# Layer 2 of a graph network: the tile order turned from low degree first to high degree first

## The chip, the cores and the metric

The kernel runs on one core of one Trainium2 chip. The metric is the device time of one execution in microseconds. A core has five engines that run their own instruction streams in order and meet through semaphores: TensorE (PE, matmuls; PEld is its weight load), VectorE (DVE), ScalarE (ACT), GpSimd (POOL) and SyncE (SP). Here POOL issues all indirect DMAs (gathers and scatters of rows by an index), and SP issues the plain ones.

## The reference, cut to what matters

Four layers run one after the other over 3125 nodes with 256 features each and 50000 edges. Each layer is a graph step and then a feed-forward step, both added to x. The change touches layer 2 and the table that layer 3 gathers from:

```python
# layer 2, graph step: attention over the incoming edges of each node
h_s = h @ W_self.T
z = h @ W_func.T
e = leaky_relu(concat([z[src], z[dst], w]) @ W_att.T)      # one score per edge
alpha = softmax of e over the edges with the same dst
h_new = h_s + segment_sum(alpha * z[src], dst)
x = x + (h + relu(where(deg > 0, h_new, h)))
# layer 2, feed-forward: 16 experts, each node goes to its best 2
gate = x_norm @ gate_w;  top 2, softmax over the two
moe = sum over the two of  w_k * (relu(x_norm @ w1[e] + b1[e]) @ w2[e] + b2[e])
x = x + layernorm(x_norm + moe) * gamma + beta
# layer 3, graph step
xp = relu(x_norm @ W_proj.T + b_proj)
agg = segment_max(xp[src], dst)                            # incoming edges and the node itself
```

## The kernel before, in words

Nodes are sorted by degree, highest first, and the sorted list is cut into 25 tiles of 128 nodes (the last, tile 24, has 53). A tile's number is its degree rank: tile 0 holds the nodes with most incoming edges. `RND` (line 90) gives the number of gather rounds of each tile, from 32 for tile 0 down to 9 for tile 24, 413 in all. One round gathers one neighbour's row for each of the 128 nodes of a tile, with one indirect DMA on POOL (`gather`, line 156).

Layer 2 stands in lines 2375 to 2579. Its work is written as generators (chains) that say which engine they need next and for how long; `Plan.run` (line 1857) plays them against a simple clock of its own and so fixes the order in which each engine's instructions are issued. Among chains that could start at about the same moment the lower rank number goes first. The chains are:

- `own_rows` (rank 0): loads each tile's own x rows into XX, on SP, at most three tiles ahead of the gathers.
- `gathers` (rank 2): the 413 gathers, in blocks of four rounds. There are nine block buffers (`g_rows`, `GR_BUFS`), and a block is free again when its rows are summed.
- `attend` (rank 0): per tile the self matmul (L2469), the scores of all rounds (L2483), the softmax, and the weighted sum, one DVE instruction per round (L2502). A tile's scores need all of its rounds, so its first block comes free only after its last gather.
- `route2` (rank 1): for groups of up to five tiles, layer norm, the gate's logits, top 2, a running count that gives each pick a place in its expert's list, and two scatters per tile (line 160) of the normed rows into the chunk's table xg.
- `ex2.tokens`, `ex2.weights` (rank 0, SP): load an expert's rows from xg once all tiles of the chunk are scattered, and the expert's 1 MB of weights (two halves, two buffers each; in the last chunk, from the third expert on, the weights go into the nine g_rows blocks once the gathers are through with them).
- `experts2` (rank 4): for each chunk the 16 experts one after the other: transposes of the rows (L2196), the hidden matmuls (L2134), relu on ACT (L2222), the output matmuls (L2138), and a store to yg.

The tiles are divided into three chunks (`CH2`, line 96: first tile, end tile, rows per block, blocks). A chunk's table has a fixed number of places per expert: 96 x 2 = 192 for the first two, 128 x 1 for the last. A token that finds no place is counted, and a branch behind the routing (`rest`, line 2299) works such tokens off; it is not taken when there are none, but every engine passes through it.

When the last group is routed, the planner's first run ends, `rest` is issued, and a second run begins in which `experts2` has rank 0. Beside the remaining experts it issues `ex2.fetch` (two gathers per tile of the expert outputs) and `table3`: combine, layer norm, layer norm again, the projection (L2549) and one scatter per tile into layer 3's table tab3. Layer 3's first gather waits for the whole of tab3; layer 3 itself walks the tiles from 0 to 24 and has its own chunks (`CH3`).

The order around the change is this: tiles 24, 23, ... 6 and then 0, 1, ... 5. Chunk 0 is tiles 15 to 24, chunk 1 tiles 6 to 14, chunk 2 tiles 0 to 5.

Of the kernel before, what the change touches and what calls it, by code (L numbers as in the profile page):

```python
# [21 lines left out]
NT = 25  # L22
# [70 lines left out]

CH2 = ((15, 25, 96, 2), (6, 15, 96, 2), (0, 6, 128, 1))
CH3 = ((0, 5, 104, 2), (5, 15, 128, 3), (15, 25, 128, 3))


# [16 lines left out]
def tile_gnn_ffn(ctx: ExitStack, tc: tile.TileContext, a: dict, out: bass.AP):  # L116
# [28 lines left out]
    def bcast(src, n, pool, name):  # L145

        t = pool.tile([P, n], F32, name=name)
        nc.sync.dma_start(t, bass.AP(tensor=src.tensor, offset=src.offset, ap=[[0, P], [1, n]]))
        return t
# [180 lines left out]
    def top2(lg, nt, n, pool, comb):  # L330
        res = {}
        for _ in top2_steps(lg, nt, n, pool, comb, res):
# [13 lines left out]
    xg2, yg2, xg3 = ([dram.tile([places(n, c) + (k[0] == "x") * 2 * P * (c[1] - c[0]), w], F32, name=f"{k}_{i}") for i, c in enumerate(ch)]  # L346
                     for k, n, w, ch in (("xg2", 16, D, CH2), ("yg2", 16, D, CH2), ("xg3", 8, D + TAIL, CH3)))

# [222 lines left out]
    class Search:  # L571
# [14 lines left out]
        def places(self, s):  # L586
            row = self.row[:, s]
            nc.vector.tensor_scalar(row, row, 1.0, None, op0=OP.max)
            nc.vector.tensor_copy(self.rowi[:, s], row)
            nc.vector.tensor_scalar(row, row, float(ET), -float(ET), op0=OP.mult, op1=OP.add)  # L590
# [142 lines left out]
    def first_zeros():  # L733
# [7 lines left out]
        yield  # L741
        for x, n in [(x, places(16, c)) for x, c in zip(xg2, CH2)] + [(x, places(8, c)) for x, c in zip(xg3, CH3)]:
            w = n // P * x.shape[1]
# [1180 lines left out]
    def norm_steps(dst, src, n, pool, pre, ready, twice=False, which=("ACT",)):  # L1924


        st = pool.tile([P, GT, 6], F32, name=pre + "st", bufs=1)
        mv = pool.tile([P, GT, 2], F32, name=pre + "mv", bufs=1)
        nm = pool.tile([P, GT], F32, name=pre + "nm", bufs=1)
        for i in range(n):  # L1930
            f = yield "DVE", 0.41, (ready[i],)
            nc.vector.bn_stats(st[:, i, :], src[:, i, :])  # L1932
            nc.vector.bn_aggr(mv[:, i, :], st[:, i, :])
        s = {}
        f = yield from small_steps(rsq_steps(s, "r", mv[:, :n, 1], n, pool, pre, 1), f)
        r = s["r"]
        if twice:
            v2 = pool.tile([P, GT], F32, name=pre + "v2", bufs=1)
            f = yield "DVE", 0.26, (f,)
            nc.vector.tensor_mul(v2[:, :n], mv[:, :n, 1], r)  # L1940
            nc.vector.tensor_mul(v2[:, :n], v2[:, :n], r)
            f = yield from small_steps(rsq_steps(s, "r", v2[:, :n], n, pool, pre + "2", 1), f)
            f = yield "DVE", 0.08, (f,)
            nc.vector.tensor_mul(s["r"], s["r"], r)
            r = s["r"]
        f = yield "DVE", 0.08, (f,)
        stt(nm[:, :n], mv[:, :n, 0], -1.0, r, op0=OP.mult, op1=OP.mult)
        done = []
        for i in range(n):
            done.append((yield which, 0.58, (f,)))  # L1950
            if plan[0].on == "ACT":
                nc.scalar.activation(dst[:, i, :], src[:, i, :], AF.Identity, bias=nm[:, i : i + 1], scale=r[:, i : i + 1])
            else:
                nc.vector.tensor_scalar(dst[:, i, :], src[:, i, :], r[:, i : i + 1], nm[:, i : i + 1], op0=OP.mult, op1=OP.add)
        return done

    def logit_steps(lg, src, g, w, b, n, ready, R, pool, name, us, *args, **kw):

        last = None
        for i in range(g + 1):  # L1960
            if i < g:
                xt = pool.tile([P, 2, P], F32, name=name, bufs=2)
                xf = yield from turned_steps(R["tp"], xt, src[:, i, :], ready[i], us, *args, **kw)
            if i:
                f = yield "PE", 0.4, (last[1], R["u"])
                free = R["u"].take()
                pl_ = ps("u", [P, 2, D])[:, 0, :n]
                for k in range(2):
                    nc.tensor.matmul(pl_, last[0][:, k, :], w[:, k, :], start=(k == 0), stop=(k == 1))  # L1969
                f = yield "DVE", 0.08, (f + slack[0],)  # L1970
                nc.vector.tensor_add(lg[:, i - 1, :], pl_, b)
                free.t = f
            last = (xt, xf)
        return f
# [400 lines left out]
    with tc.tile_pool(name="g2", bufs=2) as gp, \  # L2375
# [7 lines left out]
        bj = bcast(a["L3_gnn_b_proj"], D, wp, "w_bp")  # L2383
        ex2 = Experts("L2_ffn", 16, AF.Relu, CH2, wp, xg2, yg2)
        q2 = XX[:, :, V_Q + 1]
# [40 lines left out]
                                                   op0=OP.mult, op1=OP.add)  # L2426
        rounds_beyond(wp, body2)

        order2 = list(range(NT - 1, CH2[2][1] - 1, -1)) + list(range(CH2[2][1]))
        pl = plan[0] = Plan()  # L2430
        R = {"tp": Ring(2), "mm": Ring(2), "y": Ring(1), "u": Ring(2), "pu": Ring(1)}
        blocks = Ring(GR_BUFS)
# [3 lines left out]
        def gathers():  # L2436
            for t in order2:
                for r0 in range(0, RND[t], GB):
                    m = min(GB, RND[t] - r0)
                    for r in range(m):  # L2440
                        f = yield "POOL", 1.27, (blocks,) if r == 0 else ()
                        if r == 0:
                            g, free = gp.tile([P, GB, ZW], F32, name="g_rows", bufs=GR_BUFS), blocks.take()
                        gather(g[:, r, :], tab2, srcI[:, OFF[t] + r0 + r : OFF[t] + r0 + r + 1])
                    rows[t].append((r0, m, g, free, f))
                here[t].t = f

        def own_rows():

            for k, u in enumerate(order2):  # L2450
                old = here[order2[k - 3]] if k > 2 else At(0.0)
                while old.t is None:
                    yield None, 0.0, (old,)
                f = yield "SP", 0.45, (old,)
                nc.sync.dma_start(XX[:, u, : V_Q + 2], tabr[u * P : (u + 1) * P, : V_Q + 2])
                xin[u].t = plan[0].moved(f, 4 * P * (V_Q + 2))
# [51 lines left out]
                done[t].t = f  # L2508

        def route2():  # L2510
            for c, t0, g in ((0, 20, 5), (0, 15, 5), (1, 10, 5), (1, 6, 4), (2, 0, 4), (2, 4, 2)):
                s = slice(t0, t0 + g)
                slack[0] = SLACK if c < 2 else 0.0
                ready = yield from norm_steps(XN[:, s, :], X[:, s, :], g, gp, "rn_", [done[t] for t in range(t0, t0 + g)])
                lg = wp.tile([P, GT, 16], F32, name="r_lg")
                f = yield from logit_steps(lg, XN[:, s, :], g, rw2, gb2, 16, ready, R, gp, "r_xt", 0.36)
                yield from ex2.route(c, t0, g, lg[:, :g], f, XN, R)
                for t in range(t0, t0 + g):
                    f = yield "DVE", 0.41, (f,)
                    nc.vector.tensor_add(X[:, t, :], X[:, t, :], be)  # L2520
            moved.t = f

        def experts2():
            for c in range(3):
                yield from ex2.run(c, R)
# [32 lines left out]
        with tc.manual_schedule(engines={EN.PE, EN.DVE, EN.Activation, EN.Pool, EN.SP}):  # L2558
            pl.add(0, own_rows())
            pl.add(2, gathers())  # L2560
            pl.add(0, attend())
            pl.add(1, route2())
            pl.add(0, ex2.tokens())
            pl.add(0, ex2.weights((blocks, lambda: gp.tile([P, GB, ZW], F32, name="g_rows", bufs=GR_BUFS)
                                   .rearrange("p r d -> p (r d)"), here[order2[-1]])))
            ex2.out = "ACT"
            last = pl.add(4, experts2())
            pl.run(moved, R.values())
            ex2.out = "ACT", "DVE"
            ex2.rest(range(NT))  # L2570
            pl.meet(6.0)
            last[0] = 0
            order3 = ((20, 25), (15, 20), (10, 15), (6, 10), (3, 6), (0, 3))
            pl.add(3, ex2.fetch([t for g in order3 for t in range(*g)]))
            befores = [At(0.0), At(0.0)]
            for i, q in enumerate(order3):
                befores.append(At())
                pl.add(3 + i, table3(range(*q), f"t{i % 2}_", befores[i], befores[i + 2]))
            pl.run()
# [193 lines left out]
```

## Time and profile before

| what | value |
|---|---|
| median of 13 runs | 3167.89 us (3160.71 to 3173.7) |
| the profiled execution, its own time | 3165.59 us |
| its span, mean granted PE clock | 3163.9 us, 0.805 |
| PE, PEld, DVE, ACT, POOL busy | 2144.9, 1495.3, 1683.0, 939.7, 1699.0 us |
| layer 2: first gather issued, last gather issued | 1487.2, 2068.0 us |
| layer 3: first gather issued | 2279.7 us |
| 413 gathers of layer 2 on POOL | 404.1 us, 979 ns each |
| sum of one round on DVE (L2502) x413 | 201.5 us, 488 ns each |
| hidden matmuls of layer 2's first two chunks (L2134, 192 columns) and output matmuls (L2138) | 116.9 and 125.3 us with a few of the last chunk's |

A span runs from the first to the last instruction of the profiled execution. Times are microseconds from the span's start. "Busy" leaves out waits; a group's row ends with the idle time of the engine ahead of its instructions and with what ended that idle time. The granted clock is the share of full speed that TensorE was given. The chain that ended last is followed back from the final instruction, at each step to the work that released it.

### The profile page before, as it was taken

What the parts mean: (1) busy time and instruction counts of PE and PEld (TensorE: products, weight loads), DVE (VectorE), ACT (ScalarE), POOL (GpSimd) and SP (SyncE); (2) the same over time, 40 slices, a digit from 0 to 9 for tenths busy, and PEclk for the clock granted to TensorE, in tenths of its full rate; (3) what the DMA queues carried; (4) which work ended last, traced back from release to release, by engine and by line L of the source; (5) the groups of instructions that cost most, each with busy time, mean ns of one, the idle gap of its engine ahead of it and who ended that gap; (6) DMA issues with size and microseconds to landing.
All of it is one profiled execution on the core that took longest, in us unless ns stands there. A gap on an engine that the chain in (4) does not pass through costs nothing. (4 is left out here: it accounts for less than half of the span.)

```text
span 3163.9 us, 35848 instructions
## 1 busy us (share of the span) xinstructions
PE 2144.9 (68%) x10124; PEld 1495.3 (47%) x10124; DVE 1683.0 (53%) x6018; ACT 939.7 (30%) x2059; POOL 1699.0 (54%) x1976
## 2 busy tenths in 40 slices
PE   7999856899999999695223885968311222237898
PEld 3444324556666677574111763757201122226676
DVE  3555245677778875433757565668533333356311
ACT  3555423244444443221101331324100000024343
POOL 2210055466656710423777777754477777747644
PEclk9999976899999999797555896989555555557899
DMA  8999877578888740613433885866233333325665
GB/s 314 377 387 349 319 257 223 170 249 296 290 275 273 237 140 32 216 64 108 138 99 103 256 266 160 271 216 218 67 105 105 105 106 105 105 101 151 162 159 115
DMA packets 244652, 608.06 MB, mean 192 GB/s; under 512 B 47374, under 2 KB 111471, under 8 KB 231498
## 3 DMA queue, kind: packets, MB, share of 16 engines
q0 software_dynamic: 103824, 282.18, 29.8%
q1 hardware_dynamic: 138378, 321.21, 29.6%
q10 hardware_dynamic: 2224, 2.11, 0.2%
q8 instruction: 87, 1.43, 0.2%
q14 instruction: 139, 1.14, 0.1%
HBM read 395.45 MB, written 211.44 MB: 192 GB/s over the span
## 5 line engine op out<-in xcount | busy, mean ns | idle before, releaser
L156 POOL DMA_INDIRECT g<-part,e_code x392 | 378.2, 965 | 420.3 <-DMA f<-in_attr 201.3
L156 POOL DMA_INDIRECT g_rows<-tab,srcI x413 | 404.1, 979 | 129.2 <-issue 101.8
L156 POOL DMA_INDIRECT g_row<-tab,srcI x413 | 391.5, 948 | 131.9 <-issue 118.8
L655 PE MATMUL t<-w_big,n_xt 128*128 128x512 f32 x800 | 355.3, 601 | 11.8 <-DMA w_big<-in_L_gnn_weight 7.1
L2626 DVE TENSOR_TENSOR ACC<-ACC,g_row 128x256 f32<-128x256 f32 x413 | 175.7, 425 | 342.2 <-DMA g_row<-tab,srcI 342.1
L1790 PE MATMUL tp<-ident,ACC 128*128 128x128 f32 x50 | 16.6, 435 | 423.5 <-DVE ACC L2626 423.5
L2134 PE MATMUL mm<-ro_xt,ro_w 128*128 128x192 f32 (+3 forms) x928 | 242.9, 416 | 24.1 <-ACT ro_h L2222 14.6
L655 PEld LDWEIGHTS t<-w_big,n_xt 128*128 128x128 f32 x800 | 151.2, 192 | 195.1 <-issue 175.4
L2138 PE MATMUL y<-ro_w,ro_h 128*96 128x256 f32 (+2 forms) x1040 | 239.9, 384 | 5.0 <-ACT ro_h L2222 5.0
L1021 PE MATMUL w<-xt,w_big 128*128 128x256 f32 (+1 forms) x832 | 216.4, 393 | 0.1
L2134 PEld LDWEIGHTS mm<-ro_xt,ro_w 128*128 128x128 f32 x928 | 183.3, 218 | 69.0 <-ACT ro_h L2222 20.7
L1790 PEld LDWEIGHTS tp<-ident,ACC 128*128 128x128 f32 x50 | 7.2, 203 | 430.8 <-issue 355.3
L2502 DVE SCALAR_TENSOR_TENSOR ACC<-g_rows,g_e,ACC 128x256 f32<-128x256 f32 x413 | 201.5, 488 | 13.3
L1030 PE MATMUL w<-w_big,b_h 128*128 128x256 f32 x800 | 204.1, 392 | 2.9 <-ACT b_h L1023 2.9
L2138 PEld LDWEIGHTS y<-ro_w,ro_h 128*96 128x96 f32 (+2 forms) x1040 | 179.3, 177 | 46.3 <-ACT ro_h L2222 5.9
L893 DVE TENSOR_TENSOR g<-pw,g 128x512 f32<-128x512 f32 x196 | 126.3, 686 | 124.8 <-PE pw L889 87.7
L658 ACT COPY n_tst<-t 128x512 f32<-128x512 f32 x200 | 117.0, 586 | 190.1 <-PE t L655 183.5
L1021 PEld LDWEIGHTS w<-xt,w_big 128*128 128x128 f32 x832 | 149.5, 197 | 50.2 <-issue 27.1
L1030 PEld LDWEIGHTS w<-w_big,b_h 128*128 128x128 f32 x800 | 148.6, 193 | 38.2 <-issue 13.4
L902 PE MATMUL agg<-g,s 128*32 128x256 f32 x1568 | 140.8, 424 | 34.6 <-DMA g<-part,e_code 20.5
L2288 POOL DMA_INDIRECT out_x<-ro_y,ro_at x64 | 101.5, 1585 | 102.4 <-ACT ro_y L2251 92.5
L880 ACT COPY pw<-w_bd 128x512 f32<-128x512 f32 x196 | 112.1, 589 | 115.5 <-DVE g L893 115.0
(600 smaller groups left out, 4200.3 us busy)
## 6 DMA issues: line engine op xcount, KB each, us to landing
part<-n_tst SPq DMA_DIRECT2D x100, 1024.0 KB
ro_w<-in_L_ffn_blocks SPq DMA_DIRECT2D x58, 514.0 KB
ro_w<-in_L_ffn_blocks SPq DMA_DIRECT2D x58, 512.0 KB
part<-p_out SPq DMA_DIRECT2D x98, 256.0 KB
xg<-zero SPq DMA_DIRECT2D x78, 200.0 KB
f<-in_attr SPq DMA_DIRECT2D x49, 256.0 KB
b_at<-in_edge_attr SPq DMA_DIRECT2D x50, 224.0 KB
tabn<-v SPq DMA_DIRECT2D x11, 768.0 KB
```

The source lines that it names most:

```text
L156: return nc.gpsimd.indirect_dma_start(out=dst, out_offset=None, in_=table, in_offset=bass.IndirectOffsetOnAxis(ap=idx, axis=0))
L655: nc.tensor.matmul(pt.rearrange("p r d -> p (r d)"), xt_of[t][:, k, :], wrel[:, k, 2 * i : 2 * i + 2, :].rearrange("p r d -> p (r d)"), st ...
L658: nc.scalar.copy(stage[0][:, o : o + 2, 0, :], pt)
L880: nc.scalar.copy(pw, bd.unsqueeze(1).to_broadcast([P, 2, D]))
L893: nc.vector.tensor_tensor(m, biased.pop(0), m, op=OP.mult)
L902: nc.tensor.matmul(pa[32 * j : 32 * j + 32, h, :], s[:, 2 * j + h, :], rows[4 * g + 2 * (j // 2) + h][:, j % 2, i * D : (i + 1) * D], star ...
L1021: nc.tensor.matmul(ph, w["01"][:, e, k, i * P : (i + 1) * P], xt[:, k, : n * h], start=(k == 0), stop=(k == 1))
L1030: nc.tensor.matmul(py, last[:, k, i * h : (i + 1) * h], w["02"][:, e - 1, k, :], start=(k == 0), stop=(k == 1))
L2134: nc.tensor.matmul(ph, w[:, o : o + P], xt[:, k, :], start=(k == 0), stop=(k == 1))
L2138: nc.tensor.matmul(py, h[:, i, s], w[:, i * D : (i + 1) * D], start=(i == 0), stop=(i == self.fc - 1))
L2502: stt(u, g[:, r, :D], e[:, r0 + r : r0 + r + 1], u, op0=OP.mult, op1=OP.add)
L2626: nc.vector.tensor_tensor(u, u, rows.pop(r), op=OP.max)
```

## The change

Layer 2's tile order becomes 0, 1, ... 24, the highest degree rank first. The three chunks become tiles 0 to 8, 9 to 17 and 18 to 24, with the same numbers of places per expert as before, by position. The six routing groups and the six groups of `table3` follow the same order.

```diff
-CH2 = ((15, 25, 96, 2), (6, 15, 96, 2), (0, 6, 128, 1))
+CH2 = ((0, 9, 96, 2), (9, 18, 96, 2), (18, 25, 128, 1))
...
-        order2 = list(range(NT - 1, CH2[2][1] - 1, -1)) + list(range(CH2[2][1]))
+        order2 = list(range(NT))
...
-            for c, t0, g in ((0, 20, 5), (0, 15, 5), (1, 10, 5), (1, 6, 4), (2, 0, 4), (2, 4, 2)):
+            for c, t0, g in ((0, 0, 5), (0, 5, 4), (1, 9, 5), (1, 14, 4), (2, 18, 5), (2, 23, 2)):
...
-            order3 = ((20, 25), (15, 20), (10, 15), (6, 10), (3, 6), (0, 3))
+            order3 = ((0, 5), (5, 9), (9, 14), (14, 18), (18, 22), (22, 25))
```

## The prediction

> **What bounds the kernel now.** I read the page's slices, then the chain that ended last, then the timeline of each engine between 1480 and 2280 us, where layer 2 lies. First the chain, as it passes from layer 2's last gathers to layer 3's first:
>
> ```profile
> 2068.01 3.19 DMA g_rows<-tab,srcI
> ...
> 2075.05 31.80 DMA xg<-XX,ro_pos
> ...
> 2218.91 1.68 DMA yg<-ro_y
> ...
> 2270.36 6.90 DMA tab<-ACC,idI
> ...
> 2279.73 0.98 POOL g_row L156
> ```
>
> Up to 2068 the stage follows POOL's gathers; then it waits for the last routing group's rows (until 2108), then for PE and the last chunk's 16 experts (until 2219), then for layer 3's table (until 2279). Whatever ends that table later moves all of layer 3 by as much.
>
> Next POOL's timeline: the first gather, the last gathers of tiles 15, 10 and 6 (at 1658, 1774 and 1873; they end routing groups 2 to 4), and these groups' last scatters into xg (at 1737, 1887 and 1941):
>
> ```profile
> 1487.18 1.00 POOL L156 DMA_INDIRECT g_rows<-tab,srcI  x1 [3.58 <-DVE g_e L2480]
> ...
> 1658.35 0.94 POOL L156 DMA_INDIRECT g_rows<-tab,srcI  x1 [0.30 <-issue]
> ...
> 1737.12 0.97 POOL L160 DMA_INDIRECT xg<-XX,ro_pos  x1 [0.19 <-issue]
> ...
> 1774.18 0.95 POOL L156 DMA_INDIRECT g_rows<-tab,srcI  x1 [0.30 <-DVE g_e L2483]
> ...
> 1873.34 0.96 POOL L156 DMA_INDIRECT g_rows<-tab,srcI  x1 [0.30 <-issue]
> ...
> 1887.45 1.05 POOL L160 DMA_INDIRECT xg<-XX,ro_pos  x1 [0.19 <-issue]
> ...
> 1940.96 0.97 POOL L160 DMA_INDIRECT xg<-XX,ro_pos  x1 [0.19 <-issue]
> ```
>
> A gather takes 0.95 + 0.30 = 1.25 us of POOL, a scatter with its memset 1.3 us. The lag from a group's last gather to its last scatter is 79, 113 and 68 us for groups 2 to 4; by the same timeline it is 89 us for group 1 (1555.2 to 1643.9), 63 us for group 5 (2016.8 to 2080.1) and, for the two tiles of group 6 with nothing behind them, 41 us.
>
> Last, busy time by stretch: chunk 0's experts, the gap, chunk 1's, the gap, chunk 2's, the tail (PE, PEld, DVE, ACT, POOL, granted clock, DMA share, GB/s):
>
> ```profile
> 1742.00:1895.00 153.00, 132.53 (x661) 108.82 (x661) 88.41 (x281) 53.91 (x146) 117.97 (x129) 0.91 0.85 259
> 1895.00:1944.00 49.00, 15.21 (x46) 9.39 (x46) 33.64 (x129) 5.56 (x16) 38.34 (x47) 0.53 0.40 118
> 1944.00:2087.00 143.00, 128.01 (x640) 104.69 (x640) 88.76 (x276) 50.31 (x137) 104.51 (x115) 0.91 0.84 260
> 2087.00:2113.00 26.00, 7.12 (x24) 4.37 (x23) 11.50 (x69) 3.13 (x8) 7.00 (x10) 0.60 0.71 252
> 2113.00:2219.00 106.00, 87.06 (x506) 74.96 (x506) 81.94 (x304) 42.88 (x122) 52.28 (x66) 0.95 0.61 193
> 2219.00:2280.00 61.00, 23.82 (x62) 14.79 (x62) 32.22 (x126) 8.86 (x20) 22.89 (x34) 0.58 0.19 59
> ```
>
> The reader is to see that in the expert stretches PE is the fullest engine, and that chunk 1 ends at 2087, 26 us ahead of chunk 2's first matmul. That gap is all the slack that PE has against the last routing group.
>
> **The change, part by part.** No instruction is added: 413 gathers, 50 scatters, 48 experts of the same padded sizes (192, 192, 128 columns) stay, so every edit costs only through time and order.
>
> *Gathers in front of each chunk.* From RND, chunk 0 now needs tiles 0 to 8, 193 gathers instead of 123; chunks 0 and 1 together 333 instead of 275. Tile 0 now comes first and takes 8 of the 9 blocks. Its first block comes free 8.9 us after its last gather (1919.7 to the fourth sum at 1928.6), while POOL has only 4 gathers (5.0 us) more room: a stall of 4 us, which scatters covered before. Then:
> - chunk 0: 1487.2 + 192 x 1.253 + 4 + 10 x 1.3 = 1744.8 for its last gather, + 79 (group 2's lag) = 1824 for its last scatter, + 5.2 (1940.96 to the first matmul at 1946.15) = 1829 for PE, against 1742. With its 153 us it ends at 1982.
> - chunk 1: gather 275 at 1487.2 + 274 x 1.253 + 4 + 18 x 1.3 = 1857.9; gather 333 at 1930.6. The fourth group's last scatter comes at 1998 by its own lag of 68, or at 1858 + 113 + 54 = 2025 if the third group is as late as now and the fourth follows it by the present 54 us (1887.45 to 1940.96). I take the middle, 2010, so PE at 2015, against 1944. Bounds: not before chunk 0's end, 1982; with the longest lag (113, C's scatters ahead of it) 2057 + 5 = 2062.
> - chunk 2: the last gather lies at about 2054 (10 fewer scatters ahead of it), the last scatter between 2054 + 41 = 2095 and, by group 5's lag and the present 28 us between the last two groups, 2030 + 63 + 28 = 2121. I take 2110, against 2108. Its tiles have at most 13 rounds, so the sums behind the last gather are shorter (9 x 0.5 us instead of 19); this lies beside chunk 1's experts and is worth nothing to the end.
>
> *The work that is late next.* Chunk 1 has run 2110 - 2015 = 95 us by then, at its present pace of 143 / 16 = 8.9 us an expert: 10.7 experts. So 5.3 are left behind the last scatter, where there were none. Without gathers and attention an expert of 192 columns takes PE 6.52 us (two y groups of 16 matmuls start at 1988.24 and 1994.76 at a granted clock of 1.00): 35 us. The branch that looks for tokens over capacity stands ahead of them; its flag is there at 2105.0, and POOL, whose scatters end at 2108.0, goes on at 2109.6, SP at 2110.1, while PE has nothing to do. It now stops PE between two experts: taken as 6 us (PE's 2103.4 to SP's 2110.1, rounded down), bounds 1.6 (POOL's pause) and 9.7 (PE's present wait there, mostly for the rows). So chunk 2 starts at 2110 + 6 + 35 = 2151 instead of 2113: +38. Queued behind it are SP's weight loads of chunk 2, which come early enough as now (nine blocks, 4.5 experts ahead).
>
> The price of these experts has two ends: 35 us at the 6.52 us of the stretch at full clock, 5.3 x 8.9 = 47 us at the mean pace of chunk 1, whose row has a granted clock of 0.91 and gathers beside it (the gap before it has 0.53). I keep 35, since there are no gathers behind the last group and no gap among these experts, and 47 for the range. The Trainium skill, "TensorE: Matmul & The Clock Gate", Part 1, says that an idle window of about 3.4 us halves PE's clock and a busy one restores it; the rows' 0.53 and 1.00 agree. By that rule the pause at the branch would make the first 3.4 us after it run at half speed, an estimate of 1.7 us more; with it the sum below would be 44 instead of 42.
>
> *Layer 3's table.* Of the table matmuls of L2549, 60 (15 tiles) lie in chunk 2's stretch with 16.15 us of PE, and L1907's transposes for them take 5.76; 40 (10 tiles) lie in the tail. Now 18 tiles are ready for the longer expert stretch: 3 x (16.15 + 5.76) / 15 = +4 us of PE. The tail has 7 tiles of chunk 2 instead of 6 but perhaps no left-over group of four: +3 (two fetches more, 2 x 1.25) to -10. I take 0.
>
> *Edits at nothing.* The route's slack rule and SP's own-row loads follow the same order as before. Own rows are loaded up to three tiles ahead, hidden by tile 0's 40 us of gathers; without that cover their price is the one wait of 14.8 us that PE's transposes have for them, at the stage's start. Zeroing of xg has the same number of rows. In layer 3 tile order is untouched.
>
> **Sum.** 38 + 4 + 0 = +42 us. The profiled execution took 3165.59 us (span 3163.9 and 1.7 around it), so 3207.6; the median of the runs shown is 2.3 above it: 3210. Differences under 0.2% (6 us) are about what a measurement of this kernel can't tell from none.
>
> **Rivals.**
> - *Routing catches up* (0.17). Groups 3 and 4 are routed while PE and ACT have less to do, and chunk 1 starts as chunk 0 ends, 1982. Then 33 us more of it lies ahead: 3.7 experts x 6.52 = -24, so 3186. For it: group 4's lag of 68. Against it: group 3's 113, the one that was routed beside a running chunk of experts, as both are now.
> - *Routing is slower* (0.13). Start at 2062: 5.3 experts more left over, +34, so 3244; the slower 8.9 us price would come on top (+13 or more). For it: tiles of 16 to 32 rounds load DVE earlier; against it: DVE is at 0.6 in the expert rows.
> - *Faster* (0.07). The last group's two tiles have fewer rounds; if chunk 1 were through by the early bound, chunk 2 would start at 2100 instead of 2113: -13, + 3 for the seventh tile, so 3158. It decides only if chunk 1 starts by 2100 - 143 = 1957, 21 us after its last gather's time with the 5 us to the first matmul; the shortest lag in the trace is 41.
> - *Tokens overflow* (0.01). A chunk's share per expert may pass its capacity, and the branch then runs 16 experts over 25 tiles: at 2.3 + 1.9 us of matmuls each some 1,660 us. I evaluated the reference on its own inputs and counted: at most 172 of 192, 188 of 192 and 121 of 128 places. None overflows.
>
> **How the numbers follow.** The forecast itself (0.62) is 3210, with a range of its own from 3190 to 3235. 3186 lies within the whole range; its low end allows for the tail's -10 on top, its high end reaches 3244 and the dearer experts in part: 3174 to 3250. Faster by over 0.2%: 0.07 from the third rival, 0.01 for the first one with the tail's -10 and a still earlier start. Within 0.2%: 0.03, the low end of the first rival. Slower: the rest, 0.89.
>
> **What would show it.** Right: chunk 0's first transposes of ro_x near 1829 and chunk 1's near 2015; experts of 192 columns after the last scatter; chunk 2's first matmul of 128 columns near 2151; layer 3's first gather near 2322; the stretch from there to the end unchanged. Wrong: chunk 1 ending before about 2100, a PE gap ahead of chunk 2 as long as now, groups with lags under 50 us, or POOL stalls far above 4 us after tile 0.

## The result and the profile after

The changed kernel takes 3270.08 us in the median of 8 runs (3267.6 to 3279.9), against 3167.89 us before: a ratio of 1.0328, 95% interval 1.0316 to 1.0340, so 102 us slower. The forecast was 3210 with a range up to 3250. The direction was right, the size was not: the price was two and a half times as high.

The chain that ended last, of the changed kernel, at the same places as before (start, duration, engine):

```profile
2066.00 3.59 DMA g_rows<-tab,srcI
...
2095.56 34.29 DMA xg<-XX,ro_pos
...
2216.85 9.93 DMA yg<-ro_y
...
2324.95 1.67 DMA yg<-ro_y
...
2375.39 7.49 DMA tab<-ACC,idI
...
2385.07 0.99 POOL g_row L156
```

The gathers end 2 us earlier than before (2068.01), and yet layer 3's first gather comes at 2385.07 instead of 2279.73: +105.3. From there to the end nothing is lost: 881.9 us, against 884.2 before. So all of it lies between the last gathers of layer 2 and layer 3's first. New in the chain is a store of an expert's output (yg, 192 KB) in the middle that takes 9.93 us to land, where the last store (128 KB) takes 1.67.

POOL's timeline of the changed kernel: the last gather and the last scatter of routing groups 2, 3 and 4, in order of time, and the last scatter of group 6:

```profile
1747.69 0.95 POOL L156 DMA_INDIRECT g_rows<-tab,srcI  x1 [0.30 <-issue]
...
1828.22 0.97 POOL L160 DMA_INDIRECT xg<-XX,ro_pos  x1 [0.19 <-issue]
...
1863.78 0.95 POOL L156 DMA_INDIRECT g_rows<-tab,srcI  x1 [0.30 <-issue]
...
1938.62 1.00 POOL L156 DMA_INDIRECT g_rows<-tab,srcI  x1 [0.30 <-issue]
...
1976.27 1.24 POOL L160 DMA_INDIRECT xg<-XX,ro_pos  x1 [0.19 <-DMA g_rows<-tab,srcI]
...
2049.51 0.97 POOL L160 DMA_INDIRECT xg<-XX,ro_pos  x1 [0.19 <-issue]
...
2123.19 1.56 POOL L160 DMA_INDIRECT xg<-XX,ro_pos  x1 [0.19 <-issue]
```

The lags are 81, 112 and 111 us (before 79, 113 and 66). Groups 2 and 3 lag as they did; group 4, which releases chunk 1, lags 45 us more. The 66 are counted from the 275th gather, the last one of tile 6 before the change; the line at 1873.34 that the prediction took for it is the 274th (POOL's timeline before):

```profile
1874.61 0.95 POOL L156 DMA_INDIRECT g_rows<-tab,srcI  x1 [0.31 <-issue]
```

Busy time of the changed kernel by stretch, cut as before: chunk 0's experts, the gap, chunk 1's experts, chunk 2's, the tail. There is no stretch between chunks 1 and 2 any more (columns: length; PE, PEld, DVE, ACT, POOL busy; granted clock; DMA share; GB/s):

```profile
1834.00:1987.00 153.00, 130.27 (x667) 106.89 (x665) 95.96 (x307) 54.29 (x149) 117.88 (x130) 0.91 0.86 269
1987.00:2055.00 68.00, 22.93 (x66) 14.23 (x67) 52.56 (x192) 10.65 (x30) 53.07 (x61) 0.50 0.39 109
2055.00:2209.00 154.00, 136.73 (x708) 111.82 (x708) 80.21 (x328) 53.88 (x140) 53.36 (x74) 0.93 0.63 189
2209.00:2326.00 117.00, 80.23 (x471) 69.54 (x469) 43.55 (x162) 38.26 (x111) 27.39 (x36) 0.84 0.62 197
2326.00:2385.00 59.00, 16.07 (x44) 10.02 (x44) 30.74 (x123) 7.25 (x16) 22.34 (x29) 0.58 0.19 55
```

Against the rows of before: chunk 1 starts 109 us later (2054.74 against 1946.15) and is 13 us longer from there to its end (154 against 141); the 26 us of slack ahead of chunk 2 are gone; chunk 2 is 11 us longer (117 against 106), though it has less PE work in it (80 us busy against 87); the tail is 2 us shorter. 109 + 13 - 26 + 11 - 2 = 105. The chunk 2 row shows that something new stalls PE there. PE's and ACT's timelines of the changed kernel at that border, with the idle time ahead and what ended it:

```profile
2227.11 0.69 PE L2196 MATMUL tp<-ident,ro_x 128*128 128x128 f32 x2 [11.00 <-DMA ro_x<-xg]
...
2250.93 3.78 PE L2134 MATMUL mm<-ro_xt,g_rows 128*128 128x128 f32 x16 [19.72 <-ACT ro_xt L2204]
```

```profile
2249.15 1.58 ACT L1952 ACTIVATE ACC<-ACC,t_nnm,t_nr 128x256 f32<-128x256 f32 x3 [32.63 <-DVE t_nnm L1947]
```

PE waits 11.0 us for the rows of chunk 2's next expert, and then 19.7 us for ACT to copy transposed rows (ro_xt); ACT stands for 32.6 us in an instruction of `table3`, the norm of a group whose expert outputs are still on their way. What keeps them is seen in SP's own queue:

```profile
2209.81 5.66 SPq L2168 DMA_DIRECT2D g_rows<-in_L_ffn_blocks  x9
2216.85 0.33 SPq L2262 DMA_DIRECT2D yg<-ro_y  x1
2218.84 1.43 SPq L2148 DMA_DIRECT2D ro_x<-xg  x2
```

Nine weight loads of chunk 2 (each 0.5 MB) are issued in one burst ahead of the store of chunk 1's last output and of the rows that PE will wait for. Before the change the same burst was there (SP's queue before), but chunk 2's first rows came only at 2110, when the last group was routed:

```profile
2087.72 5.57 SPq L2168 DMA_DIRECT2D g_rows<-in_L_ffn_blocks  x9
2094.20 0.33 SPq L2262 DMA_DIRECT2D yg<-ro_y  x1
2110.10 9.78 SPq L2148 DMA_DIRECT2D ro_x<-xg  x4
```

### The profile page after: what moved, and what is told of

It is laid out like the page before. It is cut to its first block, busy times and chain, and to the rows that moved or that the text cites. A ratio compares the mean times of both kernels' runs of the same rounds, so it can differ in the third digit from the quotient of the medians.

```text
span 3267.0 us, 35829 instructions
## 1 busy us (share of the span) xinstructions
PE 2128.9 (65%) x10124; PEld 1485.8 (45%) x10124; DVE 1688.0 (52%) x6028; ACT 935.3 (29%) x2049; POOL 1696.0 (52%) x1976
## 5 line engine op out<-in xcount | busy, mean ns | idle before, releaser
L655 PE MATMUL t<-w_big,n_xt 128*128 128x512 f32 x800 | 355.2, 601 | 10.7 <-DMA w_big<-in_L_gnn_weight 8.0
L2134 PE MATMUL mm<-ro_xt,ro_w 128*128 128x192 f32 (+3 forms) x928 | 235.8, 405 | 20.4 <-ACTq L2309 5.7
L2138 PE MATMUL y<-ro_w,ro_h 128*96 128x256 f32 (+2 forms) x1040 | 241.7, 386 | 5.2 <-ACT ro_h L2222 5.2
L655 PEld LDWEIGHTS t<-w_big,n_xt 128*128 128x128 f32 x800 | 151.4, 193 | 193.8 <-issue 171.7
L2502 DVE SCALAR_TENSOR_TENSOR ACC<-g_rows,g_e,ACC 128x256 f32<-128x256 f32 x413 | 201.3, 488 | 13.5
L2134 PEld LDWEIGHTS mm<-ro_xt,ro_w 128*128 128x128 f32 x928 | 176.2, 210 | 63.0 <-ACT ro_h L2222 9.7
L2138 PEld LDWEIGHTS y<-ro_w,ro_h 128*96 128x96 f32 (+2 forms) x1040 | 180.0, 178 | 46.1 <-ACT ro_h L2222 5.6
L2469 PE MATMUL pu<-w_s,a_xt 128*128 128x256 f32 x100 | 43.4, 579 | 201.8 <-DVE ACC L2497 191.1
```

Of the source, the lines that this page charges most:

```text
L655: nc.tensor.matmul(pt.rearrange("p r d -> p (r d)"), xt_of[t][:, k, :], wrel[:, k, 2 * i : 2 * i + 2, :].rearrange("p r d -> p (r d)"), st ...
L2134: nc.tensor.matmul(ph, w[:, o : o + P], xt[:, k, :], start=(k == 0), stop=(k == 1))
L2138: nc.tensor.matmul(py, h[:, i, s], w[:, i * D : (i + 1) * D], start=(i == 0), stop=(i == self.fc - 1))
L2502: stt(u, g[:, r, :D], e[:, r0 + r : r0 + r + 1], u, op0=OP.mult, op1=OP.add)
```

## The experiments

Ratios are against the kernel before, run beside each of them on the same chip (3163 to 3166 us, but for one chip of which more below).

**1. Is it the direction, or what chunk 1 has to wait for?** `late_chunk1` is the kernel before, low degrees first, with only two tiles taken earlier; chunk 1 then waits for 331 gathers instead of 275 (the changed kernel: 333).

```diff
-        order2 = list(range(NT - 1, CH2[2][1] - 1, -1)) + list(range(CH2[2][1]))
+        order2 = list(range(24, 9, -1)) + [0, 1, 9, 8, 7, 6, 2, 3, 4, 5]
```

> The kernel before with one edit: tiles 0 and 1 (56 gathers) are taken ahead of tiles 9 to 6 instead of behind them, so chunk 1 needs 331 gathers instead of 275 and everything else (chunks, groups, sizes, low degrees first) stays. Theory 'chunk 1 is late': its first matmul moves from 1946 to between 2030 and 2060 (56 x 1.25 = 70 us and a longer lag), the 26 us gap ahead of chunk 2 is used up, and the time rises by 60 to 110 us (3228 to 3278). Rival 'it is the direction itself' (big tiles first, a last chunk of seven tiles): no change, 3158 to 3178.

Measured: 3253.76 us, ratio 1.0278 (1.0245 to 1.0311). Chunk 1's first transposes come at 2040.97, and the same stall stands at the border to chunk 2 (PE's timeline of this run):

```profile
2040.97 0.90 PE L2196 MATMUL tp<-ident,ro_x 96*128 96x96 f32 x4 [7.08 <-DMA ro_x<-xg]
...
2237.74 3.58 PE L2134 MATMUL mm<-ro_xt,g_rows 128*128 128x128 f32 x16 [18.44 <-ACT ro_xt L2204]
```

That is as expected, start and time. Two tiles moved give 88 of the 102 us, this stall included, with the low-degree chunk 0, the groups and the table order of before. So most of the price is there without the direction, once chunk 1 hangs on nearly as many gathers; the other 14 us were not taken apart.

`late_chunk0` exchanges only the first two chunks of the kernel before, so that chunk 0 waits for 152 gathers instead of 123 and chunk 1 for 275 as before:

```diff
-CH2 = ((15, 25, 96, 2), (6, 15, 96, 2), (0, 6, 128, 1))
+CH2 = ((6, 15, 96, 2), (15, 25, 96, 2), (0, 6, 128, 1))
...
-        order2 = list(range(NT - 1, CH2[2][1] - 1, -1)) + list(range(CH2[2][1]))
+        order2 = list(range(14, 5, -1)) + list(range(24, 14, -1)) + list(range(6))
```

(The routing groups and the table's groups follow.)

> The kernel before with its first two chunks exchanged: tiles 14 to 6 first (152 gathers), then 24 to 15, then 0 to 5. Chunk 0 is ready about 29 x 1.25 = 36 us later than before, chunk 1 still after 275 gathers. Theory 'only chunk 1's start counts': no change beyond 10 us, 3158 to 3178, chunk 0 starting near 1780 and ending ahead of chunk 1's start near 1945. Rival 'a late chunk 0 pushes everything behind it': plus 30 to 40 us, near 3200.

Measured: 3206.73 us, ratio 1.0125 (1.0090 to 1.0160). The theory missed; the rival's time (near 3200) came close. The same 275 gathers no longer give the same start: chunk 1's last scatter comes at 1971.7 instead of 1941.0 (89 us behind the third group's, before 54), its first transposes at 1977.28 instead of 1946.15. Its fourth group has five tiles here instead of four, and is routed beside chunk 0's experts, which began 43 us later (1785.5 against 1742.4); which of the two counts was not taken apart. So the number of gathers alone doesn't set chunk 1's start; the routing behind them does as well. Chunk 2 begins as soon as chunk 1 is through, at 2126.2, 13 us later than before, and then takes 138.8 us instead of 106, with one PE wait of 24.7 us for a table norm on ACT (PE's timeline):

```profile
2158.28 0.69 PE L1907 MATMUL tp<-ident,XX 128*128 128x128 f32 x2 [24.70 <-ACT XX L1952]
```

**2. How does it grow?** `tile0_early` takes tile 0 alone ahead (307 gathers in front of chunk 1):

```diff
-        order2 = list(range(NT - 1, CH2[2][1] - 1, -1)) + list(range(CH2[2][1]))
+        order2 = list(range(24, 9, -1)) + [0, 9, 8, 7, 6, 1, 2, 3, 4, 5]
```

> The kernel before with one edit: tile 0 alone (32 gathers) is taken ahead of chunk 1's last four tiles (tile order 24 to 10, 0, 9 to 6, 1 to 5), so that chunk 1 waits for 307 gathers; before it is 275 and the time 3166, with tiles 0 and 1 ahead it was 331 and 3254. Nothing is left out. Theory (only that part of chunk 1's delay counts which exceeds the gap ahead of chunk 2, 26 us before, and from there on it counts in full, with some 10 us on top for the border): chunk 1 starts 45 to 60 us later, at 1991 to 2006, and layer 3's gathers start 20 to 45 us later: 3186 to 3211. Rival (proportional to the gathers, with no gap: 32/56 of the 88 us that 56 gathers cost): 3211 to 3222. Second rival (the end is set by the last groups until the routing is later by more than that): 3160 to 3172.

Its first run fell on a chip on which the kernel before takes 3701 us: 3740.87 us, a ratio of 1.0110 (1.0075 to 1.0145). It was run again beside the earlier ones:

> The kernel before with tile 0 alone taken ahead of chunk 1's last four tiles, as tile0_early. Theory (only what exceeds the 26 us gap ahead of chunk 2 counts, then in full, with some 10 us for the border): chunk 1 starts at 1991 to 2006, layer 3's gathers 20 to 45 us later, 3186 to 3211 where the kernel before takes 3166. Rival (proportional to the gathers): 3211 to 3222.

Measured there: 3221.46 us, ratio 1.0186 (1.0160 to 1.0212), against 3163.03 us for the kernel before: 58 us more. That is outside the threshold's range, and inside the proportional one as a time (3211 to 3222), though 2 us above it as a difference (45 to 56). But the stretches of chunk 1 and chunk 2 show that the gap does count:

```profile
2007.00:2158.00 151.00, 129.22 (x651) 106.07 (x651) 82.97 (x309) 51.60 (x138) 83.71 (x96) 0.92 0.73 222
2158.00:2280.00 122.00, 94.11 (x532) 80.54 (x530) 67.48 (x256) 45.83 (x127) 38.28 (x55) 0.90 0.62 200
```

Chunk 1 starts 61 us later (2007.23) and is 10 us longer; 26 us of that vanish in the gap, and chunk 2 starts 45 us later. Chunk 2 is 16 us longer than before, of which the tail gives 8 back: layer 3's first gather comes 53 us later, at 2332.8, in the profiled execution (3215.4 us). So in the trace the gap is used up first, but a chunk 1 that ends against chunk 2 costs more than the 10 us that I had put on top, and the time is the rival's; from two sizes, a proportion can't be excluded.

**3. Why is the fourth group late?** In the changed kernel its norm begins only when the third group's sends are through (VectorE's timeline: the last add behind b2 of group 3, then group 4's first statistics), 43 us after its last gather was issued:

```profile
1980.11 0.42 DVE L2128 TENSOR_TENSOR ACC<-u,XX 128x256 f32<-128x256 f32 x1 [0.92 <-PE u L2126]
1982.12 0.42 DVE L1932 BATCH_NORM_STATS2 rn_st<-XX 128x6 f32<-128x256 f32 x1
```

Two explanations: VectorE is given to attention first, or routing is one serial chain. `route_first` exchanges the ranks:

```diff
-            pl.add(0, attend())
-            pl.add(1, route2())
+            pl.add(1, attend())
+            pl.add(0, route2())
```

> The changed kernel with the ranks of two chains exchanged: routing 0, attention 1, so that DVE issues routing steps ahead of sums that could start at the same moment. Theory 'the routing groups follow one another in one chain, and each is stretched by attention's sums on DVE': the fourth group's last scatter comes 15 to 40 us earlier than 2050, chunk 1 starts as much earlier, and the time falls by 10 to 40 us, to 3230 to 3260. Rival 'the lag is the gathers and the chain's own latency': no change of that lag beyond 5 us, 3262 to 3278.

Measured: 3275.70 us, ratio 1.0337 (1.0300 to 1.0375): no gain, and the fourth group's lag stays at 110 us (1946.98 to 2057.40). The rank isn't it. `split_route` lets a group's sends (scatters, transposes, products with b2) run as a chain of their own, beside the next group's norm and logits:

```diff
-            there = f + slack[0] / 2
-            last = None
+            out = self.send(c, t0, g, comb, f, residual, R, pre, slack[0], aside)
+            if aside:
+                plan[0].add(1, out)
+            else:
+                f = yield from out
+            return f
+
+        def send(self, c, t0, g, comb, f, residual, R, pre, lag, aside):
+
+            n, pool = self.n, self.pool
+            there = f + lag / 2
             for t in range(t0, t0 + g):
...
```

> The changed kernel with one edit: a group's sends (scatters of its rows, transposes and products with b2, adds into ACC) run as a chain of their own, beside the next group's norm, logits, top two and positions, instead of ahead of them. Nothing is left out. Theory (the fourth group is late because routing is one serial chain: its norm began at 1982, one microsecond or two after the third group's last scatter, although its last gather was issued at 1939): the fourth group's last scatter comes 25 to 40 us earlier (2010 to 2025, against 2049.5), chunk 1's first transposes with it (2015 to 2030, against 2054.7), the start of layer 3's gathers moves by 20 to 40 us, and the time is 3232 to 3250 (after: 3270.1). Rival (VectorE is full between 1982 and 2054, 56.7 us busy of 72, so that a second chain only takes turns with the first): the last scatter moves by under 10 us and the time stays within 3262 to 3278.

Measured: 3250.91 us, ratio 1.0257 (1.0233 to 1.0281). The norm begins at 1947.98, the last scatter comes at 2025.44, chunk 1 starts at 2031.02, 24 us earlier (timelines of VectorE, POOL and PE of this run):

```profile
1947.98 0.42 DVE L1932 BATCH_NORM_STATS2 rn_st<-XX 128x6 f32<-128x256 f32 x1
```

```profile
2025.44 0.97 POOL L160 DMA_INDIRECT xg<-XX,ro_pos  x1 [0.19 <-issue]
```

```profile
2031.02 0.90 PE L2208 MATMUL tp<-ident,ro_x 96*128 96x96 f32 x4 [8.90 <-DMA ro_x<-xg]
```

That is the serial chain shown: 19 us of the 102. It is a little less than was expected everywhere: the norm starts 34 us earlier, but the last scatter only 24 (25 to 40 expected) and layer 3's first gather 16 (2368.91; 20 to 40 expected). Probably that is because the fourth group still goes through VectorE and PE beside the attention and chunk 0's experts; this wasn't taken apart. The same edit on the kernel before:

> The kernel before with the sends split off in the same way. Nothing is left out. Before, chunk 1's fourth group had its last scatter 68 us after its last tile's gathers, and chunk 1 ended 26 us ahead of chunk 2's start, which waited for the last groups. Theory (chunk 1's start is not what sets the end of layer 2 before the change, the last groups are): chunk 1 starts 0 to 20 us earlier (1946.2 before), chunk 2 starts no more than 5 us earlier than 2113.4, and the time stays within 3158 to 3172. Rival (chunk 1's start sets the end in this order too): the time falls by as much as chunk 1's start, 10 to 20 us, to 3145 to 3157.

Measured: 3165.36 us, ratio 0.9999 (0.9984 to 1.0014). Chunk 1 starts 3 us earlier (1943.00), chunk 2 at the same moment as before (2113.38, before 2113.44). The time is the one that the theory gave, and the split brings nothing there. But 3 us are too small a shift to show what an earlier chunk 1 would do in the old order; that its end had 26 us of slack is read from the stretches of before.

**4. The border of chunks 1 and 2.** `made_late` tells the planner that chunk 1's output lands later, so that it writes the combine of it further back in VectorE's and ACT's order:

```diff
-            self.made[c].t = f + 0.5
+            self.made[c].t = f + (25.0 if self.table is None else 0.5)
```

> The changed kernel with one edit in the planner's book-keeping: it takes layer 2's expert outputs to be in memory 25 us after the last store of a chunk instead of 0.5 us, so combine and norm of layer 3's table are ordered later among the instructions of DVE and ACT. Theory 'at the border of chunk 1 and chunk 2 the experts' copies on ACT stand in order behind table work that waits for a late store': the wait of 19.7 us of PE for ACT's ro_xt copy goes, and the time falls by 15 to 35 us, to 3235 to 3255. Rival 'the border wait only takes the place of PE work that is needed anyway, or moves into the tail': within 8 us of 3270.

Measured: 3258.32 us, ratio 1.0294 (1.0258 to 1.0330). The wait of 19.7 us for ro_xt is gone, the one for ro_x is still there at 10.99 us; the gain, 12 us, is under what was expected. `two_ahead` leaves the loads ahead out:

```diff
-            pl.add(0, ex2.weights((blocks, lambda: gp.tile([P, GB, ZW], F32, name="g_rows", bufs=GR_BUFS)
-                                   .rearrange("p r d -> p (r d)"), here[order2[-1]])))
+            pl.add(0, ex2.weights())
```

> The changed kernel with one edit: chunk 2's weights are no longer loaded ahead into the free blocks of the gathers; they use the experts' own W_BUFS buffers as in chunks 0 and 1. Nothing is left out. Theory (at the border of chunk 1 and chunk 2 nine weight loads issued by SP at 2209.8 to 2215.5 stand ahead of the store of the last y and of the rows of chunk 2, so that the store needs 9.9 us to land where one later needs 1.7, and TensorE waits 11.0 us for ro_x): the store lands in 2 to 4 us, the 11.0 us wait for ro_x goes or falls below 4 us, and the time falls by 5 to 15 us, to 3255 to 3265. Rival (the ahead loads pay for themselves: chunk 2 needs its weights faster than two buffers take them): chunk 2 gets longer than its 113 us, weight waits show in TensorE's rows, and the time is 3270 to 3300.

Measured: 3252.54 us, ratio 1.0265 (1.0242 to 1.0288), some 17 us faster than the changed kernel and a little more than expected. SP's queue, POOL's first fetch, and chunk 2's stretch in this run:

```profile
2209.03 3.33 SPq L2168 DMA_DIRECT2D ro_w<-in_L_ffn_blocks  x2
2212.69 0.33 SPq L2262 DMA_DIRECT2D yg<-ro_y  x1
```

```profile
2217.51 0.98 POOL L156 DMA_INDIRECT ro_g<-yg,ro_back  x1 [15.07 <-DMA ro_x<-xg]
```

```profile
2212.00:2309.00 97.00, 81.06 (x470) 70.17 (x468) 43.26 (x164) 38.47 (x109) 27.16 (x36) 0.93 0.75 237
```

The store is issued 4 us earlier and has landed within 4.8 us (the fetch follows it at 2217.51), both long PE waits are gone (the longest left is 3.9 us), and chunk 2 takes 97 us instead of 117. Two weight buffers feed it: weights cost PE 0.6 us of idle time there. So the burst is what makes the store and the rows late. For PE's 19.7 us the early place of the table's norm in ACT's order is needed too, since `made_late` takes that wait away with the burst in place. Both edits together:

> The changed kernel with no weights loaded ahead and chunk 1's y written as 24.5 us later, without the split. Nothing is left out. Theory (both edits take away the same stall): within 5 us of the better one alone, 3247 to 3256 where the kernel before takes 3166. Rival (two costs: the loads delay the store and the rows, the early combine holds ACT and VectorE up): they add, 3236 to 3246.

Measured: 3247.72 us, ratio 1.0257 (1.0224 to 1.0291), which can't be told apart from `two_ahead` alone, but the interval leaves room for a sum of the two gains (29 us) too. The traces decide it. In the changed kernel and in these three runs nine experts of chunk 1 are left behind the branch. From PE's first matmul there to layer 3's first gather the changed kernel takes 254.1 us (2131.01 to 2385.07), `made_late` 241.0, `two_ahead` 236.4 and both together 234.0 (the changed kernel's PE; PE and POOL of `two_made`):

```profile
2131.01 1.62 PE L2134 MATMUL mm<-ro_xt,ro_w 128*128 128x192 f32 x4 [5.30 <-PEq L2309]
```

```profile
2141.10 1.62 PE L2134 MATMUL mm<-ro_xt,ro_w 128*128 128x192 f32 x4 [5.03 <-PEq L2309]
...
2375.13 0.99 POOL L156 DMA_INDIRECT g_row<-tab,srcI  x1 [5.74 <-issue]
```

The gains are 13, 18 and 20 us, far from a sum of 31: the two edits take away one and the same stall.

**5. Together, and on the kernel before.** `split_made` has the split and the later combine:

> The changed kernel with the sends split off as in the run with the split chain, and with the order written as if chunk 1's y came 24.5 us later (the edit that gave 3258.3 alone). Nothing is left out. Theory (the late fourth group and the stall at the border are two separate costs): the two gains add, about 30 us and 12 us, and the time is 3220 to 3240. Rival (an earlier chunk 1 takes the border's stall away by itself, since the table's work is then further ahead of the experts): no more than 4 us faster than the split chain alone.

Measured: 3234.06 us, ratio 1.0206 (1.0176 to 1.0236); 19 and 12 us add up to 31, 36 were found, inside the theory's range. All three edits were run first on the slower chip:

> The changed kernel with all three edits: the sends split off, chunk 1's y written as 24.5 us later, and no weights loaded ahead. Nothing is left out. Alone they gave 19, 12 and 17 us, the first two together 36. Theory (the last two edits take away the same stall at the border, so that they don't add, and the split one adds): 3228 to 3240, with layer 3's gathers still 55 us or more later than before the change. Rival (all three are separate): 3218 to 3226. In both the order itself keeps at least 50 us of the 102.

> The kernel before, with chunk 2's weights not loaded ahead. Nothing is left out. Theory (the loads ahead cost only where chunk 2 follows chunk 1 at once; before the change 26 us lie between them): 3160 to 3174. Rival (they delay the last groups' scatters and the rows too): 3150 to 3160.

> The kernel before with all three edits. Nothing is left out. Theory (each of them mends something that is late only in the changed order): within 1% and not faster, 3160 to 3190, the written delay of chunk 1's y putting layer 3's table work a little later for nothing. Rival (the end of layer 2 is bound by the same stalls in both orders): 3130 to 3155.

Measured there, with 3701.25 us for the kernel before: `all_three` 3741.99 us, ratio 1.0105 (1.0070 to 1.0141); `two_ahead_b` 3704.27 us, 1.0008 (0.9989 to 1.0026); `all_three_b` 3707.06 us, 1.0011 (0.9991 to 1.0030). On the kernel before, on that chip, the border edits and all three together bring nothing, so there is no version here that beats it. The microseconds that were expected can't be read on that chip; so `all_three` was run again:

> The changed kernel with all three edits, as all_three. Alone they gave 19, 12 and 17 us, the first two together 36. Theory (the last two take away the same stall at the border, the split one adds): 3228 to 3240 where the kernel before takes 3166, a ratio of 1.0196 to 1.0234. Rival (all three are separate): 3214 to 3226, 1.015 to 1.019.

Measured: 3227.01 us, ratio 1.0202 (1.0164 to 1.0240). Chunk 1's, chunk 2's and the tail's stretches:

```profile
2029.00:2193.00 164.00, 145.22 (x708) 117.22 (x709) 100.16 (x393) 57.37 (x151) 71.88 (x91) 0.89 0.65 196
2193.00:2288.00 95.00, 81.93 (x483) 70.41 (x481) 43.79 (x164) 38.92 (x112) 30.24 (x41) 0.96 0.75 246
2288.00:2345.00 57.00, 14.12 (x44) 9.04 (x44) 30.63 (x123) 7.25 (x16) 22.33 (x29) 0.64 0.19 56
```

43 us are won back by the medians; 59 of the 102 stay (64 against the kernel before that ran beside it). Chunk 2 and the tail are now 15 us shorter than before the change, and what stays is that chunk 1 starts at 2029 instead of 1946 and chunk 2 must wait for its end at 2193. The interval holds both the expected range and the upper part of the rival's, so the time doesn't tell whether the gains add; the traces of `two_made` do.

So the 102 us are, by the runs: about 19 from the serial routing of group 4, and about 17 to 24 from the stall at the border (`two_ahead` alone, or both border edits on top of the split: 3250.9 to 3227.0). The remainder of about 60 is what `all_three` still has; no run takes it away. Its trace says where it lies: layer 3's first gather comes at 2345.20, 65 us later than before. Chunk 1 starts 83 us later, 67 of them because the last gather that it needs, now the 333rd, comes later (1941.69 against 1874.61) and 16 because the lag is longer (82 us against 66). Chunk 1 is 23 us longer, the gap of 26 is gone, chunk 2 and the tail are 15 shorter: 83 + 23 - 26 - 15 = 65. `late_chunk1` shows that the old direction costs nearly as much with 331 gathers; whether this direction would be cheap with fewer gathers ahead of chunk 1 wasn't tried.

## Why the prediction was wrong

By its own steps, against layer 3's first gather, predicted at 2322 (2279.7 + 42) and found at 2385.1; the miss is 63 us.

- *Chunk 0's start, 1829:* 1833.73. Right. So were the lags of groups 2 and 3 that it rested on (79 and 113 taken, 81 and 112 found), and the stall behind tile 0 was small (4 us taken, 2.05 found; by tile 0's last gather before, which is the one at 1920.97 and not at 1919.7, the sum gives 1928.6 - 1921.0 - 5.0 = 2.6).
- *Chunk 1's start, 2015:* 2054.74. **This is the step that failed.** I had two figures for the fourth group's last scatter: 1998 by its own lag of 68, or 2025 by 113 + 54 behind the third, and took the middle. The second was the mechanism (experiment 3), and even its 54 us behind the third group were 73: the scatter came at 2049.51. In that piece of time VectorE was busy for 58.1 us, before for 37.9: 51 of attention's sums lie in it, before 38 (24.8 and 18.2 us); the other 13.7 us more are further VectorE work of attention and routing, which I didn't take apart. The start lies inside the bounds I had given (1982 to 2062), near the upper one. The middle of two mechanisms is no mechanism: `route2` is written as one generator, so the second could have been read from the code. (The 68, 63 and 41 us of groups 4 to 6 before are 66, 61 and 39 from the groups' last gathers to their last scatters; with 66 the first figure would lie still further off.)
- *The last scatter, 2110:* 2123.19, 13 us late. Of this 12 come from the last gather, 2066.00 instead of 2054. I had taken off ten scatters ahead of it; the groups show 36 in place of 38, two fewer. The lag behind it was right (56 taken, 57 found).
- *The branch, 6 us:* PE stood for 5.30 us. Right. The Trainium skill, "TensorE: Matmul & The Clock Gate", Part 1, was cited for 1.7 us more behind such a pause, as matmuls start at half clock after an idle window of some 3.4 us. The trace agrees: PE had stood for 5.30 us. Three stretches of 3.4 us from the first matmul behind the branch:

```profile
2131.00:2134.40 3.40, 3.39 (x12) 2.93 (x13) 0.46 (x2) 0.74 (x2) 2.71 (x3) 0.55 0.30 83
2134.40:2137.80 3.40, 3.40 (x18) 2.78 (x17) 0.87 (x2) 0.55 (x1) 2.56 (x3) 1.00 0.92 298
2137.80:2141.20 3.40, 3.40 (x23) 2.93 (x22) 1.63 (x4) 1.99 (x6) 2.49 (x4) 1.00 0.91 270
```

  A granted clock of 0.55 and then 1.00: 3.4 x 0.45 = 1.5 us.
- *The experts behind the last scatter, 5.3 x 6.52 = 35:* 78 us, and the largest term of the miss, +43. Output matmuls (L2138) of the changed kernel ahead of the branch and behind it (length; PE and PEld busy; granted clock; DMA share; GB/s):

```profile
2055.00:2125.00 70.00, 25.79 (x112) 17.54 (x112) 0.92 0.63 187
2131.00:2209.00 78.00, 33.51 (x144) 23.74 (x144) 0.94 0.65 199
```

  At 16 for each expert, 7 were done and 9 were left. The 3.7 more that were left are 24 us of it, and follow from the late start. The other 19 are the price: 8.7 us an expert, where I had 6.52 from one pair at full clock. Of that, 13.1 us are table matmuls (L2549 9.8, L1907 3.3) that the planner set beside these experts. I had put them into chunk 2's stretch. The other 6 us I didn't take apart. The 8.9 us that I kept for the range was the better number, partly by luck: it came with gathers and attention beside the experts, the 8.7 with table matmuls.
- *Chunk 2 and the table, 106 + 4:* 117, +7. The table work in it was less than predicted, and the 11 + 20 us stall that I hadn't seen was more. "Weight loads of chunk 2 come early enough" was true of the weights; that the loads would hold up the store and the rows behind them on the same queue was the effect that I missed, because in the old order 26 us lay between the two.
- *The tail, 0:* -2. Right. *Layer 3 unchanged:* right (-2).

Together 13 + 2 (behind the last scatter, up to PE's first matmul) + 43 + 7 - 2 = 63.

Of the rivals, "routing is slower" came nearest: a start at 2062 and 3244, "with the slower price on top" 3257. Its start came from a lag of 113 for the fourth group (111 found), but for another reason, VectorE's load, and it had only 0.13; that it comes near is in part luck. The serial chain stood in the main sum, as the figure that was averaged away. "Routing catches up" and "faster" fell with the start at 2054.7, far above the 1982 and 1957 that they needed. No token overflowed: the branch was not taken.

## What to carry to other kernels

A change of order is priced by the moment at which each batch of dependent work becomes ready, so read the lag behind the last input for the group that releases the batch, and read from the code whether the groups run one after the other: if they do, the next one's start is the previous one's end, not its own input plus its own lag. Slack between two stages hides more than its own length: when it closed here, a prefetch burst that had always been there came to stand ahead of a store and of rows that were now urgent, and an in-order engine (ACT) that was waiting for that store held up PE. Work that is moved from a stage with gaps into one without was better priced here by the full stage's mean pace, with all that shares the engine (8.9 us an expert; 8.7 found), than by its best pair (6.52).

## What the runs showed of the hardware

- A store of 192 KB that follows nine loads of 0.5 MB in SP's queue took 9.93 us to land (9.3 to 11.6 us in five other runs with the burst), where the stage's last store, of 128 KB and with no load in front of it, took 1.67 to 1.69. Without the burst (`two_ahead`) the same 192 KB store had landed within 4.8 us. The Trainium skill, "DMA: Bandwidth & Descriptors", Queues, rings and completion order, says that each DMA engine consumes the descriptors of a queue in the order of the queue; the late landing is in line with that, though the trace doesn't show single descriptors.
- One chip ran the same work more slowly, and the runs don't show why. The kernel before took 3701 us there against 3166; the profile from there is that of `two_ahead_b`, one edit away and as long (ratio 1.0008). The long matmuls (L655) took 604 ns there and 601 before, one gather's issue 973 ns of POOL and 979 before. The packets of the two large DMA queues kept the 16 DMA engines busy for 26.5% and 25.5% of 3711.5 us, before for 29.6% and 29.8% of 3163.9, which is 983 and 946 us against 937 and 943; so 164 GB/s instead of 192 is for the most part the same bytes over a longer span. What grew is idle time. Layer 2's gathers took 793 us from the first to the last against 581; POOL stood idle ahead of them for 280.5 us, of which 117.7 ended with a sum on VectorE (L2502), that is with a free block; before it was 129.2 and 11.0. PE stood for 42.2 us ahead of output matmuls (L2138) without a cause that the profile shows; before there was no such wait ahead of them. On that chip `all_three` costs 1.05% instead of 2.02%, and `tile0_early` 1.10% instead of 1.86%: what an order costs depends on what else is slow.
